# A cross-attention kernel on one core: the means of the output rows taken from sums that VectorE keeps while it writes the rows

## The chip, the core and the metric

The kernel runs on one core of a Trainium2 chip. A core has five engines that each work through a queue of their own: TensorE (PE in the profile; its weight loads are shown apart as PEld), VectorE (DVE), ScalarE (ACT), GpSimd (POOL) and SyncE (SP), which issues the DMAs. The engines wait for each other through semaphores. The metric is the device time of one execution in microseconds (us). The kernel before the change takes 1387.44 us, the median of three runs (1387.33 to 1389.09 us).

## The reference, cut to what matters

There are B = 64 independent items. Each has 256 rows of text `x` (512 wide) and 256 rows of context `c` (384 wide), all in float32:

```python
text_p  = x @ W_text + b_text                  # 256 x 512
audio_p = c @ W_audio + b_audio                # 256 x 512
Q = layer_norm(text_p, g1, beta1)
K = layer_norm(audio_p, g2, beta2)
alpha = softmax(Q @ K.T / sqrt(512))           # 256 x 256
h = (alpha @ audio_p) @ W_out + b_out
out = layer_norm(h + x, g_out, beta_out)       # 256 x 512

def layer_norm(x, gamma, beta):
    mu = jnp.mean(x, axis=-1, keepdims=True)
    var = jnp.mean(jnp.square(x - mu), axis=-1, keepdims=True)
    return (x - mu) * jax.lax.rsqrt(var + EPS) * gamma + beta
```

The change concerns the last line alone: the mean of each of the 256 rows of `h + x`, which the last normalisation needs.

## The kernel before, in words

An item's 256 rows lie as two tiles of 128 rows (t = 0 and 1), one row to a partition. The product of the softmax weights with the context gives `zT` (384 x 256), and the output projection multiplies it by `wao = W_audio @ W_out`, folded once at the start. The key projection and this output projection use a scheme with fewer products (class `Thirds`): sums and differences of blocks of the input are made on POOL (class `Sides`; its tiles are `csum` for the keys and `zsum` for the output), PE adds the products into four PSUM banks (`ps_m`, `ps_l`, `ps_u`, `ps_n`) in five stages, `one` to `five`, and DVE combines the banks between the stages (`after_one`, `after_three`, `after_four`). The keys and the output use the same four banks, one after the other.

An output projection ends in `leave_plus` (L573), all on DVE through the helper `dve` (L489, so its instructions stand at L490). It adds the rows of `x` and writes the finished rows `yr`: for tile 1 the middle third from `ps_n` and then the two outer thirds from `ps_n`, for tile 0 the middle third from `ps_u` and the outer thirds from `ps_l`. A third is W3 = 172 columns, so the middle (172 to 344) and the right outer third (340 to 512) overlap by four columns, and the outer thirds are written last.

The last normalisation of an item starts from these rows:

- `sums` (L779): two ACT passes over the rows, scaled by -1/512, give `nm`, minus the mean of each row (L786).
- `deviations` (L790): two ACT passes with `nm` as the bias square the rows and add up (L794); POOL then makes the reciprocal deviation `rstd` (L376 and L380, in `rstd_of`).
- `shift` (DVE, L901) subtracts the mean and multiplies by `g_out`. Inside the loop ACT multiplies by `rstd` (L915) and POOL adds `beta_out` (L919); at the end of the kernel DVE does both in `settle` (L910).

The order of the work on every engine is the order in which the program calls these methods: it is written out by hand, and an engine's queue keeps it. The main loop (L1068) runs over b = 0 to 61. A pass holds stages of several items: the key projection of item b + 2 (`k2`), the query projection of item b + 2 or b + 3, the scores and the softmax of item b, the context product of item b - 1 (`last`), the output projection of item b - 2 (`old`) and the last normalisation of item b - 3 (`settled`). Near the end of a pass `old.o.leave_plus` is called (L1220), after it `last.context_one` (PE, L1224). The next pass begins with `settled.sums()` (L1086), `k2.one()` and `k2.after_one()`, and `settled.deviations()` comes some way later (L1132). On POOL the call before the place of L1086 is `lift_rows` of the item before (L919), and the call after it is `start_products`, the `zsum` sums, which wait for ACT's copy of `zT` (L760).

After the loop the last items are finished by straight-line code (L1235 to L1336), in which PE, DVE, ACT and POOL have less to overlap. Three times the statistics of an item's rows are taken there in one go, `sums` and then `deviations`:

- `settled.statistics()` (L1247) stands behind `old.start_products()` (POOL's `zsum` sums) and ahead of `last.copy_e()` (ACT, L731), whose result `eT` is what PE's `last.context_one()` (L1257) reads.
- `old.statistics()` (L1281) stands behind `last.start_products()` (POOL) and ahead of `add_bias` (POOL, L940).
- `last.statistics()` (L1314) stands behind `at.scale_soon(1)`, whose last instruction is on POOL (`rone`, L840) and waits for DVE's `veone` (L839), and ahead of `last.shift` and `last.settle` (DVE).

Of the kernel before, what the change touches and what calls it, by code (L numbers as in the profile page):

```python
# [9 lines left out]
F32 = mybir.dt.float32  # L10
AF = mybir.ActivationFunctionType
ALU = mybir.AluOpType
# [3 lines left out]
P = 128  # L16
# [6 lines left out]
def kernel(  # L23
# [18 lines left out]
    nc = tc.nc  # L42
    ctx.enter_context(tc.manual_schedule())
    B, L, D = x.shape
    S, DA = c.shape[1:]
    H = w_text.shape[1]
    LT, ST = L // P, S // P
    DC, AC, HC = D // P, DA // P, H // P
    scale = 1.0 / math.sqrt(H)
    W3 = -(-H // 12) * 4  # L50
# [9 lines left out]
    small = ctx.enter_context(tc.tile_pool(name="small", bufs=4))  # L60
# [153 lines left out]
    def bias_parts():  # L214

        part = once.tile([P, D], F32, tag="e", name="part")
        nc.vector.tensor_scalar(part, wo_sb[:, 0, :], bac_sb[:, 0:1], None, ALU.mult)
        return part
# [109 lines left out]
    def middle(row):  # L328
        return row[:, W3 : 2 * W3]

    def ends(row):

        return bass.AP(row.tensor, row.offset, [row.ap[0], [H - W3, 2], [1, W3]])
# [155 lines left out]
    def dve(o, i0, i1, op):  # L489
        nc.vector.tensor_tensor(o, i0, i1, op)  # L490

    class Thirds(Projection):
# [25 lines left out]
        @classmethod  # L518
        def seed_with(cls, bias):
            nc.scalar.copy(cls.M, ends(bias))  # L520
# [35 lines left out]
        def after_five(self):  # L556
            u, n = self.room("u"), self.room("n", 2)
            nc.scalar.copy(u, self.U)
            nc.scalar.copy(n, self.N)
            dve(middle(self.rows[:, 0]), self.T, u, ALU.add)  # L560
            dve(ends(self.rows[:, 1]), self.M, n, ALU.add)
            self.noted = u, n

        def leave(self):
            nc.scalar.copy(ends(self.rows[:, 0]), self.L)
# [7 lines left out]
        def leave_plus(self, x, between):  # L573
            rows = self.rows
            u, n, v = self.room("u"), self.room("n", 2), self.room("d")
            dve(n, self.M, ends(x[:, 1]), ALU.add)
            dve(u, self.U, middle(x[:, 1]), ALU.add)
            dve(v, self.N0, u, ALU.add)
            between()
            dve(middle(rows[:, 1]), v, self.N1, ALU.subtract)  # L580
            dve(ends(rows[:, 1]), self.N, n, ALU.add)
            u = self.room("u")
            dve(u, self.U, middle(x[:, 0]), ALU.add)
            dve(middle(rows[:, 0]), self.T, u, ALU.add)
            dve(ends(rows[:, 0]), self.L, ends(x[:, 0]), ALU.add)

    class Fork(Projection):

# [69 lines left out]
    class Attention:  # L658
# [116 lines left out]
        def statistics(self, lo=0, n=LT):  # L775
            self.sums(lo, n)
            self.deviations(lo, n)

        def sums(self, lo=0, n=LT):  # L779

            self.nm = small.tile([P, LT], F32, tag="nm", name="nm")
            self.ssq = small.tile([P, LT], F32, tag="ssq", name="ssq")
            self.summed = range(lo, lo + n)
            for t in self.summed:
                junk = work.tile([P, D], F32, tag="junk", name="junk")
                nc.scalar.activation(  # L786
                    junk, self.y[:, t, :], AF.Identity, scale=-1.0 / D, accum_out=self.nm[:, t : t + 1]
                )
# [148 lines left out]
    def add_bias(b):  # L937
        xb = x_rows[b]
        for t in range(LT):
            nc.gpsimd.tensor_tensor(xb[:, t, :], xb[:, t, :], bao_sb, ALU.add)  # L940
# [20 lines left out]
    for a in range(AC):  # L961
        pool, tag = (work, "eT") if a else (once, "e")
# [66 lines left out]
    part = bias_parts()  # L1029
# [38 lines left out]
    for b in range(B - 2):  # L1068
        at = att[b] = att.get(b) or Attention(b)
        settled, old, last = att.pop(b - 3, None), att.get(b - 2), att.get(b - 1)  # L1070
# [12 lines left out]
            q[b + 2] = Fork(b + 2, xs.pop(b + 2), wt_blocks)  # L1083
        q2 = q[b + 2]
        if settled:
            settled.sums()  # L1086
        k2.one()
        k2.after_one()
        if b < 2:
# [146 lines left out]
    settled, old, last = att[B - 5], att[B - 4], att[B - 3]  # L1236
# [7 lines left out]
    old.o.seed()  # L1244
    at.score(0, 8)
    last.transpose_e(bank[4])
    settled.statistics()  # L1247
    last.copy_e()
    at.maxima()
    at.exponentials()  # L1250
# [27 lines left out]
    old.o.leave_plus(x_rows[B - 4], lambda: None)  # L1278
    last.o.seed()
    at.context()  # L1280
    old.statistics()  # L1281
    add_bias(B - 2)
    add_bias(B - 1)
    last.o.one()
# [26 lines left out]
    at.evict(1)  # L1311
    at.scale_soon(1)
    end.context()
    last.statistics()  # L1314
    at.shift(1)
    at.settle_beside(1)
    at.store()
# [50 lines left out]
```

## Time and profile before

| what | value |
|---|---|
| median of three runs | 1387.44 us |
| time of the profiled execution | 1388.19 us |
| span of its profile (first to last instruction) | 1386.4 us |
| PE busy | 1364.5 us, 98% |
| ACT busy | 1163.5 us, 84% |
| POOL busy | 1126.4 us, 81% |
| DVE busy | 1113.4 us, 80% |
| the two passes that make `nm` (L786, 124 of each): ACTIVATE, then ACTIVATION_READ_ACCUMULATOR | 625 and 192 ns each |
| one pass of the main loop (for instance the stretch from 600.00 to 620.84 us) | 20.84 us: PE 20.84, ACT 18.22, POOL 17.58, DVE 17.16 busy |

A page of the profile gives busy times by engine, the span in 40 slices, and the chain of work that ended last: followed back from the last instruction, at each step to what released it. A timeline lists the instructions of one engine in order: start in us, duration in us, engine, line, operation, `out<-in`, shapes, count, and in brackets the idle time before it and what ended that. "L490" is a line of the kernel, which can be that of a helper; buffers are told apart by their names.

### The profile page before, as it was taken

Reading aid. Unit: us, or ns where it says so; the run is one execution under the profiler, and the core shown is the slowest. Engines: PE = TensorE matmul, PEld = TensorE weight load, DVE = VectorE, ACT = ScalarE, POOL = GpSimd, SP = SyncE. Lnnn points to the kernel's source line nnn. Section 1 sums busy time; section 2 is a strip of 40 time slices with the busy share of each in tenths; the row PEclk is TensorE's granted clock in tenths of the full one; section 3 lists DMA queues with packets and bytes.
Section 4 is the critical chain, followed back from the end, with each engine's and each line's share of the span. In section 5 each row is a group of like instructions: output and inputs, shape, how many; then the busy total and the mean of one; then the engine's idle time right before and its main releaser. Section 6 shows DMA issues by size and latency. Waiting matters only on the chain.

```text
span 1386.4 us, 26272 instructions
## 1 busy us (share of the span) xinstructions
PE 1364.5 (98%) x7423; PEld 1245.0 (90%) x7423; DVE 1113.4 (80%) x2441; ACT 1163.5 (84%) x2933; POOL 1126.4 (81%) x1803
## 2 busy tenths in 40 slices
PE   9899999999999999999999999999999999999996
PEld 5689999999999999999999999999999999999984
DVE  5768888888888888888888888888888888888867
ACT  4578888888888888888888888888898898898883
POOL 4787888888888888888888888888888888888854
PEclk9999999999999999999999999999999999999998
DMA  9588878878878788788878778888878879787661
GB/s 222 161 241 237 245 235 242 237 242 244 242 235 248 235 237 247 226 248 246 240 234 249 236 235 247 234 239 241 247 232 248 242 231 255 228 237 240 216 214 72
DMA packets 449094, 322.00 MB, mean 232 GB/s; under 512 B 153781, under 2 KB 381621, under 8 KB 448950
## 3 DMA queue, kind: packets, MB, share of 16 engines
q1 hardware_dynamic: 448854, 320.20, 78.6%
q8 instruction: 60, 0.98, 0.3%
q14 instruction: 84, 0.69, 0.2%
q10 hardware_dynamic: 96, 0.13, 0.0%
HBM read 203.57 MB, written 116.65 MB: 231 GB/s over the span
## 4 chain that ended last, share of the span: by engine, by line
PE 95%; DVE 2%; ACT 1%; issue 0%; POOL 0%; DMA 0%; DVEq 0%; SPq 0%; ACTq 0%; POOLq 0%
PE ps_f L607 28%; PE ps_sc L676 15%; PE ps_m L506 15%; PE ps_z L742 11%; PE ps_n L506 10%; PE ps_u L506 8%; PE ps_l L506 5%; DVE yr L910 0%; PE ps_f L396 0%; DMA c<-in_ctx_dram 0%; PE ps_l L236 0%; PE ps_m L236 0%; PE ps_n L396 0%; PE ps_u L396 0%; ACT kT L481 0%
## 5 line engine op out<-in xcount | busy, mean ns | idle before, releaser
L676 PE MATMUL ps_sc<-kT,qT 128*128 128x256 f32 x1024 | 261.1, 379 | 0.5 <-ACT kT L481 0.5
L324 POOL TENSOR_TENSOR zsum<-zsum,zT 128x256 f32<-128x256 f32 x310 | 197.1, 653 | 14.6
L676 PEld LDWEIGHTS ps_sc<-kT,qT 128*128 128x128 f32 x1024 | 186.2, 190 | 18.4 <-ACT kT L481 1.5
L607 PE MATMUL ps_f<-wtsum,xsum 128*128 128x256 f32 x756 | 186.4, 382 | 1.1 <-ACT ps_f L618 0.6
L324 POOL TENSOR_TENSOR zsum<-zT 128x256 f32<-128x256 f32 x124 | 73.4, 592 | 140.1 <-ACT zT L760 135.3
L742 PE MATMUL ps_z<-eT,c 128*128 128x256 f32 x768 | 186.3, 379 | 0.0
L324 POOL TENSOR_TENSOR csum<-csum,cT 128x256 f32<-128x256 f32 x310 | 173.3, 568 | 10.0
L742 PEld LDWEIGHTS ps_z<-eT,c 128*128 128x128 f32 x768 | 143.1, 190 | 17.1 <-issue 0.5
L607 PEld LDWEIGHTS ps_f<-wtsum,xsum 128*128 128x128 f32 x756 | 139.0, 191 | 16.8 <-ACT ps_f L618 1.7
L380 POOL TENSOR_TENSOR rstd<-ve,nhalf 128x2 f32<-128x2 f32 x192 | 136.3, 710 | 16.0
L919 POOL TENSOR_TENSOR yr<-yr,beo 128x512 f32<-128x512 f32 x118 | 148.0, 1278 | 0.0
L481 ACT ACTIVATE kT<-kT,columns 128x256 f32<-128x256 f32 x256 | 139.6, 595 | 0.4 <-DVE kT L75 0.4
L481 ACT ACTIVATE qT<-qT,columns 128x256 f32<-128x256 f32 x256 | 138.8, 592 | 0.0
L607 PE MATMUL ps_f<-wt,xT 128*128 128x256 f32 x504 | 130.0, 380 | 0.0
L693 ACT ACTIVATE e<-ps_sc,nmx 128x256 f32<-128x256 f32 x128 | 59.5, 470 | 67.4 <-DVE nmx L686 67.4
L901 DVE SCALAR_TENSOR_TENSOR yr<-yr,nm,go 128x512 f32<-128x512 f32 x124 | 103.6, 837 | 0.0
L607 PEld LDWEIGHTS ps_f<-wt,xT 128*128 128x128 f32 x504 | 93.5, 191 | 10.3 <-issue 0.3
L490 DVE TENSOR_TENSOR ps_l<-ps_m,t 128x172 f32<-128x172 f32 x248 | 85.7, 346 | 16.9
L490 DVE TENSOR_TENSOR ps_f<-ps_f,s 128x256 f32<-128x256 f32 x126 | 54.5, 432 | 48.4 <-PE ps_f L607 45.4
L794 ACT ACTIVATE junk<-yr,nm 128x512 f32<-128x512 f32 x124 | 87.8, 711 | 0.0
L915 ACT ACTIVATE yr<-yr,rstd 128x512 f32<-128x512 f32 x118 | 84.5, 716 | 0.0
L442 ACT ACTIVATE kr<-kr,rstd 128x512 f32<-128x512 f32 x126 | 84.0, 719 | 0.0
(229 smaller groups left out, 3777.2 us busy)
## 6 DMA issues: line engine op xcount, KB each, us to landing
kd<-kr SPq DMA_DIRECT2D x64, 512.0 KB, 3.0
kq<-kd SPq DMA_DIRECT2D x256, 128.0 KB, 3.0
qd<-qr SPq DMA_DIRECT2D x64, 512.0 KB, 3.3
qq<-qd SPq DMA_DIRECT2D x256, 128.0 KB, 2.7
xq<-in_x_dram SPq DMA_DIRECT2D x252, 128.0 KB, 3.3
x<-in_x_dram SPq DMA_DIRECT2D x63, 512.0 KB, 4.4
out_dram<-yr SPq DMA_DIRECT2D x62, 512.0 KB, 3.9
cq<-in_ctx_dram SPq DMA_DIRECT2D x252, 96.0 KB, 3.4
```

What stands on the lines that cost most here:

```text
L324: nc.gpsimd.tensor_tensor(*step)
L380: nc.gpsimd.tensor_tensor(r, ve, nhalf[:, :n], ALU.pow)
L481: nc.scalar.activation(self.T[:, k, :], self.T[:, k, :], AF.Identity, bias=bet[:, k : k + 1], scale=gam[:, k : k + 1],)
L490: nc.vector.tensor_tensor(o, i0, i1, op)
L506: nc.tensor.matmul(place, lhsT=self.sides.of[n], rhs=self.weights[n], start=(n == 14), stop=True, skip_group_check=True,)
L607: nc.tensor.matmul(place, lhsT=side, rhs=w, start=False, stop=True, skip_group_check=True)
L676: nc.tensor.matmul(self.sc[:, t, :], lhsT=self.qT[:, k, bass.ts(t, P)], rhs=self.kT[:, k, :], start=(k == 0), stop=(k == HC - 1),)
L742: nc.tensor.matmul(ps, lhsT=c_rows[self.b][:, s, bass.ts(j, P)], rhs=self.eT[:, s, :], start=(s == 0), stop=(s == ST - 1),)
L794: nc.scalar.activation(junk, self.y[:, t, :], AF.Square, bias=self.nm[:, t : t + 1], accum_out=self.ssq[:, t : t + 1],)
L901: nc.vector.scalar_tensor_tensor(row, row, self.nm[:, t : t + 1], go_sb, ALU.add, ALU.mult)
L915: nc.scalar.mul(self.y[:, t, :], self.y[:, t, :], self.r[t])
L919: nc.gpsimd.tensor_tensor(self.y[:, t, :], self.y[:, t, :], beo_sb, ALU.add)
```

## The change

The four instructions in `leave_plus` that write the rows become `scalar_tensor_tensor` instructions (the first operand times 1.0, then the same addition or subtraction) with `accum_out`: the sum of what an instruction writes goes to one element per partition of a new tile `totals` (128 x 2 x 2). So that no column is summed twice, the middle part is now 168 columns wide (`inner`, W1 = 512 - 344), and no longer overlaps the outer thirds. A new method `totals` makes `nm` from them on POOL, one 128 x 1 `tensor_scalar` for each of the two tiles: the sum of the two parts, times -1/512. It is called where `sums` was called; `deviations` stays as it is. The `sums` passes are left out for the 62 items whose rows come from `leave_plus`; the last item of all, `end`, keeps its own.

```diff
+    W1 = H - 2 * W3
+
+    def inner(row):
+        return row[:, W3 : W3 + W1]
...
             between()
-            dve(middle(rows[:, 1]), v, self.N1, ALU.subtract)
-            dve(ends(rows[:, 1]), self.N, n, ALU.add)
+            self.totals = small.tile([P, 2, 2], F32, tag="totals", name="totals")
+            self.last_sum(1, 0, inner, v[:, :W1], self.N1[:, :W1], ALU.subtract)
+            self.last_sum(1, 1, ends, self.N, n, ALU.add)
             u = self.room("u")
             dve(u, self.U, middle(x[:, 0]), ALU.add)
-            dve(middle(rows[:, 0]), self.T, u, ALU.add)
-            dve(ends(rows[:, 0]), self.L, ends(x[:, 0]), ALU.add)
+            self.last_sum(0, 0, inner, self.T[:, :W1], u[:, :W1], ALU.add)
+            self.last_sum(0, 1, ends, self.L, ends(x[:, 0]), ALU.add)
+
+        def last_sum(self, t, n, part, i0, i1, op):
+            nc.vector.scalar_tensor_tensor(
+                part(self.rows[:, t]),
+                i0,
+                1.0,
+                i1,
+                ALU.mult,
+                op,
+                accum_out=self.totals[:, n, t : t + 1],
+            )
...
+        def totals(self):
+
+            self.nm = small.tile([P, LT], F32, tag="nm", name="nm")
+            self.ssq = small.tile([P, LT], F32, tag="ssq", name="ssq")
+            self.summed = range(LT)
+            t = self.o.totals
+            for j in range(LT):
+                nc.gpsimd.tensor_scalar(
+                    self.nm[:, j : j + 1], t[:, 0, j : j + 1], t[:, 1, j : j + 1], -1.0 / D, ALU.add, ALU.mult
+                )
...
         if settled:
-            settled.sums()
+            settled.totals()
...
     last.transpose_e(bank[4])
-    settled.statistics()
+    settled.totals()
+    settled.deviations()
     last.copy_e()
...
-    old.statistics()
+    old.totals()
+    old.deviations()
...
     end.context()
-    last.statistics()
+    last.totals()
+    last.deviations()
```

## The prediction, made before the changed kernel was run

> **What bounds the kernel now.** I read the page first: the busy times, then the chain that ended last.
>
> ```profile
> PE 1364.5 (98%) x7423; PEld 1245.0 (90%) x7423; DVE 1113.4 (80%) x2441; ACT 1163.5 (84%) x2933; POOL 1126.4 (81%) x1803
> PE 95%; DVE 2%; ACT 1%; issue 0%; POOL 0%; DMA 0%; DVEq 0%; SPq 0%; ACTq 0%; POOLq 0%
> ```
>
> PE carries 95% of the chain. The other engines could be on it only at the start and the end, so I asked next for busy times in three stretches (columns: stretch, its length, then busy us and instructions of PE, PEld, DVE, ACT, POOL, then granted clock, DMA share, GB/s).
>
> ```profile
> 100.00:1300.00 1200.00, 1200.00 (x6683) 1116.77 (x6682) 988.14 (x2192) 1049.54 (x2650) 1008.70 (x1611) 1.00 0.82 241
> 1300.00:1386.40 86.40, 72.25 (x368) 60.87 (x366) 63.56 (x131) 55.75 (x142) 48.65 (x71) 0.95 0.46 149
> ```
>
> From 100 to 1300 us PE is never idle and its clock is 1.00. No product is removed, so the loop cannot become shorter; it can only become longer, if DVE makes PE wait. The last 86.4 us are another stage: PE idles for 14 us, and the order of the queues decides. So the prediction has two questions: does DVE's added work fit in the loop's slack, and what does the new order cost at the end?
>
> **What is removed.** Two ACT passes for each of 62 items. By their group a pass is an ACTIVATE of 625 ns and a READ_ACCUMULATOR of 192 ns, and in the timeline the second ACTIVATE starts 0.62 us after the first, so 2 x 0.62 = 1.24 us of ACT's time per item. In the loop this buys nothing: the ACT copy of `zT` (L760) that follows waits for PE anyway (0.21 us idle), and PE is full.
>
> **What DVE gains in work.** The timelines of DVE, PE and POOL around `leave_plus`, in one pass of the loop:
>
> ```profile
> 667.31 0.33 DVE L490 TENSOR_TENSOR yr<-d,ps_n 128x172 f32<-128x172 f32 x1
> 667.68 0.52 DVE L490 TENSOR_TENSOR yr<-ps_n,n 128x344 f32<-128x344 f32 x1
> ...
> 668.47 0.34 DVE L490 TENSOR_TENSOR yr<-ps_u,u 128x172 f32<-128x172 f32 x1
> 668.84 0.52 DVE L490 TENSOR_TENSOR yr<-ps_l,x 128x344 f32<-128x344 f32 x1
> 669.54 0.34 DVE L542 COPY n<-ps_n 128x172 f32<-128x172 f32 x1 [0.18 <-PE ps_n L506]
> 669.91 0.34 DVE L490 TENSOR_TENSOR ps_u<-ps_n,n 128x172 f32<-128x172 f32 x1
> ```
> ```profile
> 668.76 0.75 PE L506 MATMUL ps_n<-wa,csum 128*128 128x172 f32 x4
> ...
> 670.79 0.46 PE L506 MATMUL ps_u<-wa_thirds,csum 128*128 128x172 f32 x2
> ```
>
> Four terms, for one item:
> - The form: a scalar_tensor_tensor from PSUM takes 740 ns for 512 columns (L820), a tensor_tensor 678 ns (L405, qr). 0.05 us more each.
> - The accumulator's read. No DVE row has one; I suppose that it is an instruction of its own, as ACT's rows are. From below, ACT's read fits in the overlap of its neighbours: 0.09 us a time (the read at 669.97, the next ACTIVATE at 670.06). From above, its whole 0.19 us. The nearest rows are DVE's own tiny instructions: RECIPROCAL of 2 elements starts 0.12 us before the next. I take 0.12.
> - The overlap of four columns goes: middle and outer thirds are 0.37 us apart at 0.33 us of work, whereas an independent successor starts 0.09 us before the end (0.43 apart at 0.52, the outer thirds and the next). Twice 0.13 us saved, at best.
> - Sum: 4 x (0.05 + 0.12) - 2 x 0.13 = 0.42 us, which I take. Bounds: -0.26 (nothing added) and 4 x (0.05 + 0.19) = 0.96 us (nothing saved).
>
> Who waits behind it? First, `k2.one` overwrites `ps_n` at 668.76; DVE's last read of it ends at 668.20. At the end of the kernel the same wait shows 0.14 us from DVE's end to PE's start (1352.43 to 1352.57), so the slack is 0.56 - 0.14 = 0.42 us, of which some 0.15 are used (half of the sum, less the last read). Second, `k2.three` at 670.79 adds to `ps_u`, which DVE's `after_one` finishes at 670.25: slack 0.54 - 0.14, plus DVE's own idle 0.18, is **0.58 us**. Third, `after_three` and `after_six` come later and have 0.6 us or more again (0.63 us idle at 673.08). So 0.42 fits in 0.58, and the loop stays at 20.84 us. Without that cover each us beyond 0.58 would cost 60 us over the 60 passes.
>
> The Trainium skill (Vector Engine (DVE) Microarchitecture Reference, Points that are easy to get wrong) speaks against the change: such an instruction with two SBUF sources that are not bf16 is said to run at half rate, since no port is left for the accumulator. Each of the four has one source in PSUM, and L901, with two float32 sources in SBUF but no accumulator, is at best as fast as L820 (743 against 740 ns). If the rule held here, an item's 1024 columns at 1.04 ns would add 1.07 us, DVE would be (0.42 + 1.07 - 0.58) x 60 = 55 us too late over the loop, and the sum would be 1447 us.
>
> **What POOL gains.** Two 128 x 1 instructions. The nearest rows, L429 and L376, span 0.19 to 0.75 us each; I take 0.27 (the second pair of L429). In the loop they fall behind `lift_rows`, in an idle stretch of 2.14 us before `zsum`:
>
> ```profile
> 671.44 0.73 POOL L324 TENSOR_TENSOR zsum<-zT 128x256 f32<-128x256 f32 x1 [2.14 <-ACT zT L760]
> ```
>
> They start at 669.36 + 0.42 + 0.07 = 669.85 and end by 670.5 (671.4 at the upper bound), before 671.44. `nm` is needed by ACT at 673.50. Cost in the loop: nothing.
>
> **The end of the kernel.** Here POOL's queue is the trouble: `sums` waited for DVE alone, `totals` waits for whatever stands before it on POOL.
>
> ```profile
> 1340.92 0.57 ACT L731 COPY eT<-ps_f 128x512 f32<-128x512 f32 x1
> ```
> ```profile
> 1341.73 0.45 POOL L324 TENSOR_TENSOR zsum<-zT 128x128 f32<-128x128 f32 x1
> ...
> 1371.63 1.00 POOL L840 TENSOR_TENSOR rone<-veone,nhalf 128x1 f32<-128x1 f32 x1 [6.14 <-DVE veone L839]
> 1372.71 0.21 POOL L376 TENSOR_SCALAR ve<-ssq 128x2 f32<-128x2 f32 x1
> ```
> ```profile
> 1342.39 1.89 PE L742 MATMUL ps_z<-eT,c 128*128 128x256 f32 x8
> ```
> ```profile
> 1374.13 2.40 DVE L910 SCALAR_TENSOR_TENSOR yr<-yr,rstd,beo 128x512 f32<-128x512 f32 x2 [0.59 <-POOL rstd L380]
> ```
>
> 1. `settled` (L1247). The rows are there at 1336.31, but `totals` is queued behind `zsum`, which ends at 1342.18. First total 1342.26 to 1342.53; ACT's deviations from 1342.60, 1.41 us for two (as before, 1339.51 to 1340.92); behind them in ACT's queue `copy_e`, now 1344.01 to 1344.58 instead of 1340.92 to 1341.49; behind that PE's `context_one`, at 1344.7 instead of 1342.39. **+2.3 us** (2.2 to 2.8). The chain that ended last runs through this product, PE's `three` and then DVE without a gap from 1344.61 to 1353.87, so all of it is kept.
> 2. `old` (L1281). POOL is idle here and the totals are as quick as the sums were. What is left is DVE's part: PE's `one` at 1352.57 waits for the read of `ps_n`: **+0.15 us** (0 to 0.25).
> 3. `last` (L1314). DVE works without a gap from 1356.88 to 1373.5, so `leave_plus` costs its full **+0.42 us** (-0.26 to 0.96). Then `totals` stands behind `rone`, which ends at 1372.63. First total to 1372.98; both deviations to 1374.56 (before: 1372.51); POOL's `ve` at 1374.63 instead of 1372.71; `rstd` and DVE's `settle` later by the same: **+1.9 us** (1.5, if `rstd` takes the 0.70 us that it takes elsewhere instead of 1.09, to 2.9). DVE's last 12 us all stand behind `settle`.
>
> Sum: 2.3 + 0.15 + 0.42 + 1.9 = **+4.8 us** (3.4 to 6.9). On the profiled execution that is a span of 1386.4 + 4.8 = 1391.2, and with the 1.8 us around it 1393.0. That execution lies 0.75 us above the median; by the median of the runs I forecast **1392.2 us**.
>
> **The rivals.**
> - *The loop stalls.* DVE's addition passes 0.58 us and PE waits in `k2.three`. For it: the read's price is unknown, and the slack is thin. Against it: DVE's tiny rows. At 0.77 us it costs 0.19 x 60 = 11 us, at 0.96 us 23 us: 1394 to 1417, say 1404.
> - *Not slower: the totals come early at the end.* If the two totals ran on POOL as soon as their rows are ready, ahead of the last three `zsum` sums and of `rone`, terms 1 and 3 would lose their waits and +0.6 us would be left: 1388.0. The point from which it decides: both totals done by 1340.2, so that `copy_e` ends before PE needs it at 1342.3. Against it: everywhere else in the trace POOL's order is that of the calls (`ve` after `zsum`, `add_bias` after `rstd`).
> - *The change doesn't do what it says:* the sums cost VectorE much more, as with a halved rate: 1447.
> - *Faster.* Only if ACT's 1.24 us per item lay on the chain in the last 60 us more than once; the chain there shows PE, DVE and POOL.
>
> **The numbers.** What a measurement here can tell from no change is 0.2%, 2.8 us. Forecast (loop unchanged, the end later) 0.58; loop stalls 0.25; halved rate or worse 0.03; totals early, 0.10; faster 0.04. Slower 0.58 + 0.25 + 0.03 = 0.86, within 0.2% 0.10, faster 0.04. The likeliest case's own range is 1390.8 to 1394.3. The range goes up to the stalled loop's bound, 1417, and down to 1390, which leaves out the early totals, the faster case and the halved rate, 0.17.
>
> **What would show it.** Right: the stretch 100 to 1300 us still all PE; ACT busy some 100 us less and DVE some 25 us more; `nm` on POOL behind `zsum` near 1342.3, PE's `context_one` waiting for ACT's `eT` copy, `settle` of `last` waiting longer for `rstd`. Wrong: a pass longer than 20.84 us with PE waiting for DVE `ps_u`, or deviations at the end that start as early as before.

## The result, and the profile after

The changed kernel takes 1393.04 us (median of 7 runs, 1391.31 to 1394.60); the kernel before, run beside it, 1388.30 us (7 runs, 1387.33 to 1389.10). The ratio is 1.0033 with a 95% interval of 1.0022 to 1.0043: slower by 4.7 us, between 3.1 and 6.0. The forecast was 4.8 us, 1392.2.

The profiled execution took 1394.60 us, the slowest of the seven, with a span of 1392.8 us. From its page, the busy times and the chain that ended last:

```profile
PE 1365.2 (98%) x7423; PEld 1244.4 (89%) x7423; DVE 1106.2 (79%) x2689; ACT 1088.3 (78%) x2685; POOL 1159.4 (83%) x1927
PE 93%; DVE 2%; DMA 2%; ACT 1%; SPq 1%; POOL 1%; issue 1%; DVEq 0%; ACTq 0%; POOLq 0%
```

ACT has lost 75 us of work, POOL gained 33, and DVE has 7 us *less* in spite of 248 more instructions. No engine's total tells where 4.7 us come from. The busy times by stretches (columns as before: stretch, length, PE, PEld, DVE, ACT, POOL, clock, DMA share, GB/s) do:

```profile
100.00:1300.00 1200.00, 1198.71 (x6673) 1114.88 (x6673) 980.11 (x2423) 977.78 (x2415) 1037.43 (x1723) 1.00 0.81 241
1300.00:1392.80 92.80, 74.69 (x370) 62.44 (x368) 64.15 (x148) 51.22 (x126) 52.05 (x80) 0.93 0.43 140
```

PE is as full in the loop as it was. The 1.29 us that it idles there all lie between 100 and 120 us, where the first passes wait for DMAs; from 140 to 1300 us PE is busy for 1160.00 us in both kernels. The loss is in the last stretch. In these lines of ACT's, POOL's, PE's and DVE's timelines it can be seen happening, first behind the loop, then 35 us later:

```profile
1342.97 0.72 ACT L822 ACTIVATE junk<-yr,nm 128x512 f32<-128x512 f32 x1 [4.25 <-POOL nm L803]
...
1344.39 0.56 ACT L748 COPY eT<-ps_f 128x512 f32<-128x512 f32 x1
...
1377.55 0.72 ACT L822 ACTIVATE junk<-yr,nm 128x512 f32<-128x512 f32 x1 [3.43 <-POOL nm L803]
```
```profile
1342.11 0.46 POOL L324 TENSOR_TENSOR zsum<-zT 128x128 f32<-128x128 f32 x1
1342.67 0.51 POOL L803 TENSOR_SCALAR nm<-totals 128x1 f32<-128x1 f32 x2
...
1376.17 1.00 POOL L868 TENSOR_TENSOR rone<-veone,nhalf 128x1 f32<-128x1 f32 x1 [5.93 <-DVE veone L867]
1377.25 0.51 POOL L803 TENSOR_SCALAR nm<-totals 128x1 f32<-128x1 f32 x2
```
```profile
1345.01 2.74 PE L759 MATMUL ps_z<-eT,c 128*128 128x256 f32 x8 [2.07 <-ACT eT L748]
```
```profile
1380.72 2.40 DVE L938 SCALAR_TENSOR_TENSOR yr<-yr,rstd,beo 128x512 f32<-128x512 f32 x2 [0.87 <-POOL rstd L385]
```

Twice POOL's `nm` stands behind other work of POOL's queue, once behind the last `zsum` and once behind `rone`; both times ACT idles for it (4.25 and 3.43 us); the first time PE then waits 2.07 us for the `eT` copy, which stands behind the deviations in ACT's queue. So far the trace agrees with the prediction. It shows coincidence of waits, though, not what the time would be without them; the experiments show that.

One thing in this profile was not foreseen: behind its 2.07 us wait PE made the eight products in 2.74 us, which took 1.89 us before. The granted clock from 1345.00 to 1349.60 us is 0.63; before the change it was 1.00 from 1340 to 1355 us.

To compare profiles I use one more measure. From the twelve `ps_z` products with which the loop goes over into the end (1333.09 us before the change, 1333.45 after) to the last instruction, here called the stretch, it was 53.31 us before and is 59.35 us after. Spans are given to 0.1 us, so stretches are good to about 0.05 us. This leaves out the first 140 us, where the first passes wait for DMAs and from which the profiles of kernels with the same start come out up to 4 us apart.

### The profile page after: what moved, and what is told of

It is laid out like the page before. It is cut to its first block, busy times and chain, and to the rows that moved or that the text cites. A ratio compares the mean times of both kernels' runs of the same rounds, so it can differ in the third digit from the quotient of the medians.

```text
span 1392.8 us, 26399 instructions
## 1 busy us (share of the span) xinstructions
PE 1365.2 (98%) x7423; PEld 1244.4 (89%) x7423; DVE 1106.2 (79%) x2689; ACT 1088.3 (78%) x2685; POOL 1159.4 (83%) x1927
## 4 chain that ended last, share of the span: by engine, by line
PE 93%; DVE 2%; DMA 2%; ACT 1%; SPq 1%; POOL 1%; issue 1%; DVEq 0%; ACTq 0%; POOLq 0%
PE ps_f L624 26%; PE ps_m L511 15%; PE ps_sc L693 15%; PE ps_z L759 11%; PE ps_n L511 10%; PE ps_u L511 8%; PE ps_l L511 5%; SPq L72 1%; DMA qd<-qr 1%; POOL zsum L324 1%; DMA eq<-ed 1%; PE ps_f L401 0%; DMA c<-in_ctx_dram 0%; DVE yr L938 0%; PE ps_m L236 0%
## 5 line engine op out<-in xcount | busy, mean ns | idle before, releaser
L777 ACT COPY zT<-ps_z 128x256 f32<-128x256 f32 x64 | 23.8, 372 | 87.1 <-PE ps_z L759 87.1
```

## The experiments

Two theories. **Queue theory:** the loss is made at the end alone, at the two places where `totals` stands behind other work in POOL's queue; the loop loses nothing. **Rival:** VectorE's accumulating instructions, or POOL's totals in the loop, cost the time. The move of the first totals (in e1, e3 and e11) and that of the last (in e2, e3 and e11):

```diff
+    settled.totals()
     old.start_products()
...
-    settled.totals()
     settled.deviations()
     last.copy_e()
```
```diff
     last.o.leave_plus(x_rows[B - 3], lambda: None)
+    last.totals()
...
-    last.totals()
     last.deviations()
```

**e1, the first totals early.**

> The two POOL totals of the first item after the loop stand ahead of the zsum sums instead of behind them; all else as in the changed kernel (1393.0 us; before 1388.3). Queue theory (the loss is made where totals stand behind other work on POOL): PE's context_one no longer waits for the eT copy (2.1 us in the profile of the changed kernel), and what followed that wait goes too: 2.3 to 4.2 us less, so 1388.8 to 1390.7. Rival (VectorE's accumulating instructions cost the time, spread over the loop): no change, 1393.0 +- 0.5.

Measured 1389.20 us (before, beside it: 1388.34), ratio 1.0011 (1.0002 to 1.0020). PE's `context_one` has no wait any more. The stretch is 55.30 us.

**e2, the last totals early.**

> The two POOL totals of the last item but two stand right behind its leave_plus, ahead of rone, instead of behind rone. Queue theory: deviations start where the sums stood before, settle waits 1.9 us less: 1391.1. Rival (VectorE's instructions, spread over the loop): 1393.0 +- 0.5.

Measured 1391.81 us, ratio 1.0033 (1.0020 to 1.0046); the stretch is 55.58 us. The times alone could not tell this run from the changed kernel: its five times reach from 1389.81 us, the profiled one, to 1394.92 us.

**e3, both.**

> Both moves together. Queue theory: the whole loss goes, and leave_plus is 0.2 us shorter than before the change: 1388.0 (within 0.5 of the kernel before). Rival: 1393.0 +- 0.5. If the two losses hide each other only in part, between them.

Measured 1387.87 us, ratio 1.0001 (0.9992 to 1.0010); the stretch is 53.31 us, as in the kernel before. PE's `context_one` has no wait:

```profile
1340.50 1.89 PE L759 MATMUL ps_z<-eT,c 128*128 128x256 f32 x8
```

The loss is gone, with every accumulating instruction in place. Against this run the two places can be priced by the stretches: the first 55.58 - 53.31 = 2.27 us, the last 55.30 - 53.31 = 1.99 us. These prices are those of the profiled executions. By the medians e1, which still pays the last place, lies 0.3 to 2.8 us above the kernel before, an interval that holds 1.99; e2, which still pays the first, lies 2.8 to 6.4 us above it, somewhat more than 2.27, and no trace shows what its slower executions lost.

**e4, the loop alone**, and **e5, the end alone**: `sums` is put back at all three places after the loop (first diff, of which one place is shown), or in the loop (second diff).

```diff
-    settled.totals()
-    settled.deviations()
+    settled.statistics()
```
```diff
-            settled.totals()
+            settled.sums()
```

> The change in the loop alone: after the loop the three batches of statistics are ScalarE's passes again; VectorE still accumulates everywhere. Queue theory: 1388.1 (as before, within 0.5). Rival (VectorE's instructions or POOL's totals cost the loop): 1393.0.

> The other half alone: in the loop ScalarE's two passes make the means again, after the loop POOL's totals do; VectorE accumulates everywhere. Queue theory: the whole loss stays, 1393.0 (4.7 us over before, +-0.7). Rival (the loop's totals or the lighter ScalarE make the loss): 1388.3.

Measured: e4 1388.44 us, ratio 1.0002 (0.9993 to 1.0011), stretch 52.94. e5 1392.68 us (before, beside it: 1387.64), ratio 1.0041 (1.0028 to 1.0053), stretch 57.59. So the loss is made at the end: 57.59 - 53.31 = 4.28 us.

**e6, the accumulating instructions alone.** Both replacements of e4 and e5 together: nobody uses the sums.

> VectorE's accumulating instructions alone: the sums are kept and nobody uses them, ScalarE's passes make the means everywhere. Queue theory: leave_plus is 0.2 us shorter than before and hidden in the loop: 1388.1 (within 0.5 of before). Rival (the accumulating form costs the time): 1393.0.

Measured 1387.88 us, ratio 1.0002 (0.9993 to 1.0011), stretch 53.16 us. With e4 the rival has fallen: neither the accumulating instructions nor POOL's totals in the loop cost more than the 1.5 us that the intervals leave open. DVE's timeline of a pass of the changed kernel shows where the form stays free:

```profile
667.68 0.33 DVE L594 SCALAR_TENSOR_TENSOR yr<-d,ps_n 128x168 f32<-128x168 f32 x1
667.93 0.08 DVE L594 DVE_READ_ACCUMULATOR yr<-d,ps_n 128x1 f32 x1
667.93 0.51 DVE L594 SCALAR_TENSOR_TENSOR yr<-ps_n,n 128x344 f32<-128x344 f32 x1
668.37 0.08 DVE L594 DVE_READ_ACCUMULATOR yr<-ps_n,n 128x1 f32 x1
...
669.91 0.34 DVE L547 COPY n<-ps_n 128x172 f32<-128x172 f32 x1 [0.40 <-PE ps_n L511]
```

The read of the accumulator has a row of its own, 0.08 us. This agrees with the Trainium skill ("VectorE: DVE Perf Modes", section "Two Vector instructions with no wait between them": an op that also writes out its accumulator is two instructions). The row starts at the same time as the next main instruction, inside the overlap, and pushes nothing back. The middle and the outer thirds start 0.25 us apart instead of 0.37; the prediction expected this of thirds that no longer overlap, but the form changed with them, and the two were not tried apart. DVE's idle time before `n` has grown from 0.18 to 0.40 us.

**e10 and e8, one and three spare additions of 128 x 344** at the end of every `leave_plus`, to see how far the rival was from coming true:

```diff
             self.last_sum(0, 1, ends, self.L, ends(x[:, 0]), ALU.add)
+            for _ in range(3):
+                dve(self.room("spare", 2), self.L, n, ALU.add)
```

> Three spare additions of 128 x 344 from ps_l at the end of every leave_plus, 0.43 us each from start to start: VectorE is 3 x 0.43 - 0.22 = 1.07 us later than before at after_one. If the slack that the prediction counted (0.58 us) is right, PE waits 0.49 us in each of 60 passes: about 29 us more, 1422. If the slack is larger than 1.1 us: 1393 to 1395 (only the end is later by about 1.3 to 2.6).

> One spare addition of 128 x 344 behind every leave_plus instead of three: VectorE reaches after_one 0.3 us later than before the change (0.51 - 0.22). If PE's slack there is the 0.58 us of the prediction, which the run with three (0.73 us more a pass) fits, the loop does not change: 1393 to 1394. If any lateness of VectorE costs the loop: three gave 46 us over the changed kernel, so one would give 15: 1408.

Measured: one, 1392.75 us (ratio 1.0034, 1.0022 to 1.0046; PE busy for all of the 1200 us from 100 to 1300). The one addition just fills DVE's idle time: the copy of `n` starts 3.39 us after the start of `leave_plus` (665.51 to 668.90), 3.40 us before the change (666.14 to 669.54), not 0.3 us later as expected. So this run uses up nothing of the part of the slack that is PE's. Three, 1439.13 us (ratio 1.0368, 1.0352 to 1.0384), 46 us over the changed kernel and 17 more than I expected. PE's timeline with three:

```profile
690.38 0.53 PE L511 MATMUL ps_u<-wa_thirds,csum 128*128 128x172 f32 x2 [0.50 <-DVE ps_u L495]
...
711.95 0.53 PE L511 MATMUL ps_u<-wa_thirds,csum 128*128 128x172 f32 x2 [0.50 <-DVE ps_u L495]
```

A pass takes 711.95 - 690.38 = 21.57 us, 0.73 more than 20.84, and 60 times that is 44 us. The three additions, which all write the same tile, take 1.53 us up to the copy of `n` instead of 3 x 0.43 = 1.29. That copy now starts 4.45 us after the start of `leave_plus`; before the change the last write ended after 3.22 us, and 0.18 us of idle time followed. Of these 1.23 us the slack of 0.58 takes its part, and 0.65 us of delay are left; another 0.08 us passes until the products behind the wait stand as close as before (0.37 us from `three` to the next group instead of 0.29). The slack that the prediction counted was right within that 0.08 us; the price of the additions was not.

**e7, PE kept busy during the wait.**

```diff
     at.reciprocals()
+    keep_busy(10)
     last.context_one()
```

> The changed kernel with ten products of ones (128 x 128, about 2.2 us) on PE in front of the context_one that waits for the eT copy, into a bank that nobody reads then. If PE's slower products behind that wait (8 in 2.74 us against 1.89 before, granted clock 0.76) come from PE having stood idle, they run at full clock again: 1.0 to 2.0 us less, 1391.0 to 1392.0. If they have another cause, or the wait alone is the loss: 1393.0 to 1393.3.

Measured 1392.50 us (ratio 1.0033, 1.0021 to 1.0046). The eight products took 1.99 us, but that proves nothing: they took 1.99 us in e2, e5, e8 and e10 as well, where PE stood idle for the same 2.07 us. The time fell between the two ranges and decides nothing.

**e9, the changed kernel once more.**

> The changed kernel once more, for its profile. If the lower clock behind PE's 2.1 us wait (8 products in 2.74 us) belongs to that wait, it is there again and the stretch from the 12 ps_z products ahead of the end to the last instruction is 59.3 us, as in the first profile. If it was chance, the 8 products take 1.99 us as in three experiments with the same wait, and the stretch is 57.6 us, as in the kernel with the change at the end alone.

Measured 1394.28 us, one execution. Its PE timeline:

```profile
1346.38 1.99 PE L759 MATMUL ps_z<-eT,c 128*128 128x256 f32 x8 [2.07 <-ACT eT L748]
```

The stretch is 1392.5 - 1334.85 = 57.65 us; the 1334.85 us ahead of it are 1.4 us more than in the first profile. So 59.35 - 57.65 = 1.7 us of the first profile belong to a drop of the clock that came in one of six profiles with this wait. What brings it about stays open.

**e11, a version that goes further.** To both early moves it adds one: POOL makes `rstd` of `last` ahead of `rone`.

```diff
-    at.scale_soon(1)
     end.context()
     last.deviations()
+    at.scale_soon(1)
```

> Both early moves, and rone behind the reciprocal deviations of the last item but two on POOL, so that settle waits for neither. Queue theory: settle starts when DVE's shift ends, 0.6 us earlier than in the kernel with both moves: 52.7 instead of 53.3 us from the 12 ps_z products to the end; the time 1387.3, not to be told from before. Rival (rone is needed as early as settle): no gain, 53.3 us or more.

Measured 1384.96 us (before, beside it: 1387.82), ratio 0.9984 (0.9975 to 0.9993): faster than both kernels, and by more than expected. The stretch is 51.67 us, 1.64 less than in e3. DVE's two `settle` instructions, first in e3, then in e11:

```profile
1372.37 2.40 DVE L938 SCALAR_TENSOR_TENSOR yr<-yr,rstd,beo 128x512 f32<-128x512 f32 x2 [0.59 <-POOL rstd L385]
```
```profile
1371.27 1.42 DVE L938 SCALAR_TENSOR_TENSOR yr<-yr,rstd,beo 128x512 f32<-128x512 f32 x2
```

The wait of 0.59 us is gone, as expected. The pair itself is shorter by 0.98 us, which I had not counted. In e3 POOL adds `beo` to another row beside it (1372.31 to 1373.57); in e11 that addition has moved behind it (1372.58 to 1373.85, after the second `settle` is all but done):

```profile
1371.20 0.55 POOL L868 TENSOR_TENSOR rone<-veone,nhalf 128x1 f32<-128x1 f32 x1
1372.58 1.27 POOL L876 TENSOR_TENSOR y<-y,beo 128x512 f32<-128x512 f32 x1 [0.83 <-ACT y L875]
```

The Trainium skill has a rule for this ("SBUF — State Buffer", section "Who interferes with whom"): a VectorE instruction with two SBUF inputs contends with a GpSimd instruction that reads SBUF. It agrees with these rows: 2.40 us beside the 128 x 512 addition, 1.42 without. That the contention is the cause was not tried by itself.

## Why the prediction was right, step by step

- *The loop cannot get shorter, and doesn't get longer.* Right: PE is busy from 140 to 1300 us without a gap in both kernels, and e4 and e6 stand at 1.0002 of the kernel before.
- *DVE's added work, +0.42 us an item (-0.26 to 0.96).* The sign was wrong; the truth lies at the lower bound, -0.22 us. Two of the three sizes were off: the form costs nothing (329 ns for 168 columns against 332 for 172, and 510 against 516 for 344; the 740 against 678 ns that I used came from an instruction with a scalar per row, not a constant), and the read 0 instead of 0.12 us each. The saving of 0.13 us a pair was right in size (0.12), whatever made it. It did no harm: the bound held, and the predicted 0.42 as well as the measured -0.22 fit in the slack of 0.58 us, whose size e8 bears out. The upper bound of 0.96 would not have fitted.
- *POOL's totals in the loop, free.* Right: 267 ns each (0.27 assumed), in the idle time before `zsum`, which went from 2.14 to 1.54 us.
- *End, place 1: +2.3 us.* 2.27 us by e2 against e3. The chain was as told: `zsum`, `nm`, deviations, `eT` copy, `context_one`. On top of it the first profile alone shows the clock drop.
- *End, place 2: +0.15 us.* The size was near, the path wrong. `one` starts 3.95 us after the twelve `ps_z` products ahead of it before the change (1348.62) and 4.07 us after them in the changed kernel (1353.03), and likewise in e1 to e6. But it is not DVE's read of `ps_n` that it waits for now; it is POOL's `zsum`, whose five sums took 3.55 us before and 3.78 after. Why they are longer is open.

```profile
1352.57 0.82 PE L506 MATMUL ps_n<-wao,zsum 128*128 128x172 f32 x4 [1.20 <-DVE yr L490]
```
```profile
1357.10 0.82 PE L511 MATMUL ps_n<-wao,zsum 128*128 128x172 f32 x4 [1.32 <-POOL zsum L324]
```

- *End, place 3: +0.42 + 1.9 us.* `leave_plus` costs nothing there: it is 0.21 us shorter, but the two `shift` instructions ahead of it are 0.21 us longer (3.20 us instead of 2.99), so `veone` comes as long after `one` as before (18.84 and 18.83 us). `totals` behind `rone` costs 1.99 us by e1 against e3. That `rstd` would take 0.70 instead of 1.09 us was the lower case and came true; POOL's `ve` took 0.75 us instead of 0.21 and gave it back. (The 1372.51 that the prediction gives for the end of the deviations before leaves out their last read, which ends at 1372.60; its sum does not use it.)
- *Sum: 4.8 us.* The two queue places are 4.3 us by the profiles (e5 against e3) and the median moved by 4.7 (3.1 to 6.0). The mechanism, totals that stand behind other work of POOL's queue, was right and carries 4.2 of the 4.8 us. That the sum came within 0.1 us of the median is luck: of the 0.57 us of its terms for DVE 0.42 did not come, 0.12 came by another path in place of 0.15, and the interval of the measurement is 2.9 us wide.
- *What would show it.* "ACT busy some 100 us less, DVE some 25 more" was wrong on both counts: 75 less, as 62 items at 1.24 us would have told, and 7 less.
- *The rivals.* The loop did not stall, and the halved rate did not come (510 ns for 344 columns). The totals that come early were not what the kernel did, but their price, 0.6 us over the kernel before, lies within e3's interval (-1.1 to 1.4 us).

## What to carry to other kernels

When work moves to another engine, look first at what stands before it in that engine's queue and what stands behind its consumer, not at how long it takes: here two instructions of 0.27 us on GpSimd cost about 2 us at each of two places and delayed nothing at 60 others. In the loop, which PE fills, a lighter load on ACT was worth nothing; the price and the gain showed at the end of the kernel, where no engine is full. A call in such a place is cheap to move, and the version with the moves (e11) turned a loss of 4.7 us into a gain of 2.9 us by the medians (0.07% to 0.25%) and of 1.6 by the stretch.

## What the runs showed of the hardware that was not expected

- `scalar_tensor_tensor` with a constant and an accumulator, one operand in PSUM, takes as long as a `tensor_tensor` (510 ns for 344 columns against 516); the accumulator's read has a row of 82 ns that delays nothing behind it.
- Behind a PE wait of 2.07 us the granted clock fell to 0.63 for 4.6 us in one of six profiles and stayed at 1.00 in the others.
- Two VectorE instructions of 128 x 512 with both tensors in SBUF took 1.42 us together with no such GpSimd addition beside them and 2.40 us beside one. In the kernel before, L901's pair took 1.41 us (at 1372.13) and, beside a run of such additions (L940), 2.99 us (at 1357.96). That the neighbour is the cause was not tried by itself.
